# Small loads off the input's queue, one early layer-norm group, explicit attention buffers and fewer or more unread products in the seams

## The chip, the core and the metric

The kernel runs on one NeuronCore of a Trainium2 chip. The core has five engines that run side by side and wait for each other through semaphores: TensorE (PE, matrix products into PSUM), VectorE (DVE), ScalarE (ACT), GpSimd (POOL) and SyncE (SP, which here only starts DMAs). DMAs can be started by SP, ACT and POOL; each of the three has a queue of its own, and an engine issues its instructions in order. The metric is the device time of one execution in microseconds (us), over several runs.

## The reference

The input x is one image of 256 x 256 positions with 32 channels. Four layers follow, each adding its result to x; each first applies a group norm (16 groups of two channels, mean and variance over the whole image).

```
x = x + L0(_gn(x))     # layer norm over 32 channels, then attention
    a = softmax(a, axis=2)
    o = g * einsum('bstih,bsihc->bsihc', a, v)   # g = sigmoid(mn @ Wg), v = mn @ Wv
    o @ Wo + bo
x = x + L1(_gn(x))     # 3x3 average, then Sobel magnitude sqrt(gx^2 + gy^2 + eps)
x = x + L2(_gn(x))     # the same again
x = x + L3(_gn(x))     # two-layer LSTM-like recurrence, 256 sequences of 256 steps
```

In the einsum of layer 0 the softmax weights are summed over the very axis along which they add up to one, so attention is `g * v`: Wq and Wk don't reach the result. Layer 3 needs the group norm of the whole image before its first step.

## The kernel before

All 64 blocks of four image columns lie in SBUF as `xa`, 128 partitions (4 columns x 32 channels) by 256 rows. The work is done on 32 pairs of blocks (128 x 512 elements), in stages:

1. **Load** (lines 187 to 259). SP loads x in two halves of 16 columns and seven tiles `nat` of 32 columns, two DMAs each (L200). PE turns each pair with four transposes (L248), ACT copies it to `xa` (L255), DVE takes its statistics (L256). In the same SP queue, after the fourth tile, stand sixteen small loads (L205, L210): the layer norm's gamma and beta and the weights wv and wg, each four times for the four partition groups; and after all of x the constants kt (L211), mean_of (L213) and two rows for a later test (L721, L722). POOL's queue has bo, bout (L114) and wo (L126). POOL copies mean_of into `avg` (L217), then scales wv and wg by gamma (L221); PE multiplies the scaled weights (L228, L239) after the seventh tile of x.
2. **Group norm and layer norm** (lines 265 to 377). DVE aggregates the statistics (L267), PE averages them over groups (L270, L278), and DVE subtracts the mean from each pair (`shifted`, L285). Eight groups of four pairs follow: PE centres (L347), ACT squares (L370), PE sums the squares of the group before into `pvar`, one PSUM bank (L328). Groups below EARLY = 2 get their root and reciprocal ahead of the others, inside group EARLY + 1 at its third square (L338, L361); right there SP starts the DMAs that spread rows 0 to 2 of the reciprocal over partitions (`rows`, L306, four DMAs per pair), DVE shifts the last four pairs, does `norm_test` (L730 to L733), and the first three pairs are scaled (`scaled`, L316, on DVE for pair 0, else on POOL). The other groups' reciprocal (L377) comes after the last group.
3. **Attention** (lines 380 to 502). For each pair k, a list `plan` gives a time for every operation: eight gate products g and eight value products v (L432, 32 rows of PE each), ACT's sigmoid `sg` (L441), DVE's `mu` = (v + bias) x sg (L445), the output products `pr` and `pb` (L458), the residual `r` (L473, L474) and the statistics (L477). All pairs' operations are sorted by k x 5.9 + time and issued in that order. The sg tiles come from a pool of 8 buffers, the mu results `o` from one of 11. PSUM banks are handed out by `take` from a list of free ones. SP's DMAs for rows of pair 3 onward (`spread_out`) and the loads of the recurrent weights (L744, L749) are in its queue behind the first rows.
4. **Two Sobel layers** (lines 515 to 695). Each begins with `shift`: DVE aggregates (L554), PE averages the mean (L556) and the variance (L564). `busy(n)` puts n products of 128 x 256 ahead of, between and behind them; their results are read by nobody (L552). Then pairs pass through fifteen operations by a list of times; `mixed` is PE's part (L639), `residual` adds to the image (L656).
5. **The seam and the recurrence** (lines 702 to 1212). `group_norm` (L150 to L169), again with unread products (L140), then `finish` (L859 to L899), which makes the recurrence's bias rows: `sb` from the scale (L861) and the bias (L864), products `pgs` (L869), ACT's copy fx (L876), DVE's three-part split to fb (L882, L884), and pk (L889, L890). Then 256 steps whose order is a list of times with period 7.6; at its head two unread products (L1152), then the first bias products (L1037, L1040).

Stages 1 to 3 lie in one region in which every engine keeps the order of the program (`manual_schedule`), each Sobel layer and the recurrence in one of their own; `group_norm` and `finish` of stage 5 are outside, where a scheduler orders each engine's instructions.

Of the kernel before, what the change touches and what calls it, by code (L numbers as in the profile page):

```python
# [18 lines left out]
S = 256  # L19
T = 256  # L20
C = 32
# [40 lines left out]
def net_kernel(  # L62
# [47 lines left out]
    def per_channel(v, name):  # L110

        t = cp.tile([P, 1], F32, name=name)
        for j in range(J):
            nc.gpsimd.dma_start(out=t[j * C : (j + 1) * C, :], in_=v.rearrange("(c o) -> c o", o=1))  # L114
        return t

    gamma4 = cp.tile([P, 1], F32, name="gamma4")
    beta4 = cp.tile([P, 1], F32, name="beta4")
    bo4 = per_channel(b_o, "bo4")
    bout4 = per_channel(b_out, "bout4")  # L120

    wv4 = big2.tile([P, D], F32, name="wv4")
    wg4 = big2.tile([P, D], F32, name="wg4")
    wbias = cp.tile([P, 2, 2], F32, name="wbias")
    wo = cp.tile([P, D // P, C], F32, name="wo")
    nc.gpsimd.dma_start(out=wo, in_=w_o.rearrange("(k p) c -> p k c", p=P))  # L126
# [4 lines left out]
    def table(func, after):  # L131

        t = small.tile([P, 1], F32, name="table")
        nc.scalar.activation(t, after, func, scale=0.0, bias=one)
# [44 lines left out]


    avg = mp.tile([P, GROUPS, GROUPS, J], F32, name="avg")
    flag = cp.tile([1, 1], mybir.dt.int32, name="flag")
    stats = new_stats()
    def pair(t, k):
# [6 lines left out]
    with tc.tile_pool(name="nat", bufs=7, side="right") as natp, tc.tile_pool(  # L191
# [3 lines left out]
        for i, wl in enumerate(WIDTHS):  # L195
            name, bufs = ("nat", 7) if wl == 32 else ("half", 2)
            nat = natp.tile([P, 2, wl, C], F32, name=name, bufs=bufs)
            nats.append((nat, w0, wl))
            for h in range(2):
                nc.sync.dma_start(out=nat[:, h], in_=x_nat[:, h, w0 : w0 + wl, :])  # L200
            w0 += wl
            if i == 3:
                for t, v in ((gamma4, ln_gamma), (beta4, ln_beta)):
                    for j in range(J):
                        nc.sync.dma_start(  # L205
                            out=t[j * C : (j + 1) * C, :], in_=v.rearrange("(c o) -> c o", o=1)
                        )
                for t, w in ((wv4, w_v), (wg4, w_g)):
                    for j in range(J):
                        nc.sync.dma_start(out=t[j * C : (j + 1) * C, :], in_=w)  # L210
        nc.sync.dma_start(out=kt, in_=consts[:, 3:NK, :])  # L211
        mean_of = mp.tile([P, P], F32, name="mean_of")
        nc.sync.dma_start(out=mean_of, in_=consts[:, K_AVG, :])  # L213
        gb = norm_weights(tc, mp, gn_gamma, gn_beta)
        nc.gpsimd.memset(avg, 0.0)
        for g in range(GROUPS):
# [79 lines left out]
    def pair(t, k):  # L296
        return t[:, 2 * k : 2 * k + 2, :].rearrange("p b s -> p (b s)")

    EARLY = 2
    rstds = [lnp.tile([P, 2 * S], F32, name=f"rstd{i}") for i in range(2)]  # L300

    def rows_of(k):
# [15 lines left out]
    with tc.tile_pool(name="lnq", bufs=9) as lnq:  # L318
        with tc.tile_pool(name="ps_ln", bufs=7, space=PSUM) as ps_ln, tc.tile_pool(
# [22 lines left out]
            for g in range(GROUPS):  # L342
                pcs = [ps_ln.tile([P, 2 * S], F32, name="pc") for _ in range(J)]
                for j in range(J):
                    rows = slice(j * C, (j + 1) * C)
                    for r in range(J):
                        nc.tensor.matmul(  # L347
                            pcs[j][r * C : (r + 1) * C, :],
                            lhsT=cen[rows, rows],
                            rhs=pair(xb, J * g + r)[rows],  # L350
                            start=True,
                            stop=True,
                        )
                if g == 0:
                    for k in range(J, NST - J):
                        shifted(k)
                sqs = []
                for j, pc in enumerate(pcs):
                    if g == EARLY + 1 and j == 2:
                        std = deviations()  # L360
                        nc.vector.reciprocal(rstds[0], std)  # L361
                        for k in range(3):
                            rowsets[k] = rows_of(k)
                        for k in range(NST - J, NST):
                            shifted(k)
                        norm_test(tc, mp, flag, gb)
                        for k in range(3):
                            scaled(k)
                    sqs.append(lnq.tile([P, 2 * S], F32, name="sq"))
                    nc.scalar.activation(sqs[-1], pc, AF.Square)  # L370
                if g:
                    variance(g - 1, last)
                last = sqs
# [47 lines left out]
    with tc.tile_pool(name="at", bufs=3) as atp, tc.tile_pool(  # L421
        name="ps_at", bufs=1, space=PSUM
    ) as ps_at:
        free = list(range(8))
        held, sbuf = {}, {}

        def one_of(o, u, j, k):
            bias = lambda i: wbias[:, i, u : u + 1]
# [8 lines left out]
                    stop=True,  # L437
                )
            elif o == "sg":
                sg = sbuf["sg", u, j, k] = atp.tile([P, 2 * S], F32, name="sg", bufs=8)  # L440
                nc.scalar.activation(sg, held["g", u, j, k][1], AF.Sigmoid, bias=bias(1))  # L441
                release(("g", u, j, k))
            elif o == "mu":
                gated = sbuf["o", u, j, k] = atp.tile([P, 2 * S], F32, name="o", bufs=11)
                nc.vector.scalar_tensor_tensor(  # L445
                    gated,
                    held["v", u, j, k][1],
                    bias(0),
                    sbuf.pop(("sg", u, j, k)),
                    ALU.add,  # L450
                    ALU.mult,
                )
# [1 line left out]
            elif o in ("pr", "pb"):  # L454
                half = o == "pb"
                po = held["po", k][1] if half else take(("po", k))
                for i in range(J):
                    nc.tensor.matmul(  # L458
                        po[i * C : (i + 1) * C, :],
                        lhsT=wo[:, half, :],  # L460
                        rhs=sbuf.pop(("o", half, i, k)),
                        start=not half,
                        stop=half,
                    )
# [50 lines left out]
    def sobel_layer(src, dst, moments, before, after, between):  # L515
# [167 lines left out]
        with tc.manual_schedule():  # L683
            shift()
            for _, k, part, args in todo:
                part(k, *args)
                if part is twos and k == 0:
                    deviation()
                if part is statistics and between:
                    between.pop(0)(lambda: flat(ps_s.tile([P, 2, S], F32, name="pg1")))  # L690
        stack.close()
        return stats

    stats = sobel_layer(xa, xb, stats, 7, 16, [rw.selectors])
    stats = sobel_layer(xb, xa, stats, 3, 16, rw.products())
    second.close()

# [4 lines left out]
    inputs = RecurrentInputs(tc, ctx, xa)  # L702
    plain = nc.values_load(flag, min_val=0, max_val=1)
    with tc.tile_pool(name="ps_n", bufs=1, space=PSUM) as ps_n:
        gn = group_norm(stats, ps_n, 1, 0, 3)
        table(AF.Sigmoid, gn[0])
        weights = rw.finish(lw, ps_n, gn)
    with tc.If(plain > 0) as arms:
        recurrence(tc, out, ident, weights, inputs, None)
    with arms.Else():  # L710
# [25 lines left out]
class RecurrentWeights:  # L736
# [117 lines left out]
    def finish(self, lw, psum, gn):  # L854

        nc = self.nc


        for g in range(2):  # L859
            cols = slice(g * C, (g + 1) * C)  # L860
            nc.vector.tensor_scalar(  # L861
                self.sb[0:C, 0, cols], self.ident[0:C, 0:C], gn[0][0:C], None, ALU.mult
            )
        nc.vector.tensor_copy(self.sb[0:C, 1, :], gn[1][0:C].to_broadcast([C, 2 * C]))  # L864
        fx = lw.tile([P, G], F32, name="fx")
        pgs = [psum.tile([P, G], F32, name=f"pg{i}") for i in range(2)]
        for i in (1, 0):
# [103 lines left out]
def recurrence(tc, out, ident, weights, inputs, general):  # L971
# [222 lines left out]

    for k in range(inputs.NX, NB // inputs.XT):
        at(((k - inputs.NX + 1) * inputs.XT * J + 4.0) * PERIOD, inputs.load, k)
    at(-1e5, busy, 2)
    for n in range(min(ahead.values()), T + max(ahead.values())):
        at(n * PERIOD + OUT["x"], project, n)
    for t in range(T):  # L1200
# [53 lines left out]
```

## Time and profile before

| | us |
|---|---|
| median of 3 runs | 2545.38 (2543.13 to 2545.64) |
| the profiled execution | 2544.43 |
| its span, first to last instruction | 2542.6 |
| end of the load stage (last L255 copy) | 46.0 |
| attention's first product (L432) | 76.9 |
| first Sobel aggregation (L554) | 322.0 |
| second Sobel aggregation | 446.3 |
| aggregation before the recurrence (L150) | 573.5 |
| first product of the recurrence (L1037) | 586.7 |

The page of a profile gives the busy time of each engine and, in forty equal slices, the busy share in tenths; PEclk is the clock that TensorE was granted, in tenths of full speed, and DMA the busy share of the sixteen DMA engines. The chain that ended last is followed back from the last instruction, at each step to what released it. A line of a timeline has the start, the duration, the engine, the line of the kernel, the operation, its output and inputs, the count of merged instructions and, in brackets, how long the engine stood idle before it and what ended that. An engine's name with a q is its instruction queue, which issues DMAs. A product of 32-bit operands of 512 or 256 columns appears as two MATMUL instructions.

### The profile page before, as it was taken

Reading aid. Unit: us, or ns where it says so; the run is one execution under the profiler, and the core shown is the slowest. Engines: PE = TensorE matmul, PEld = TensorE weight load, DVE = VectorE, ACT = ScalarE, POOL = GpSimd, SP = SyncE. Lnnn points to the kernel's source line nnn. Section 1 sums busy time; section 2 is a strip of 40 time slices with the busy share of each in tenths; the row PEclk is TensorE's granted clock in tenths of the full one; section 3 lists DMA queues with packets and bytes.
Section 4 is the critical chain, followed back from the end, with each engine's and each line's share of the span. In section 5 each row is a group of like instructions: output and inputs, shape, how many; then the busy total and the mean of one; then the engine's idle time right before and its main releaser. Section 6 shows DMA issues by size and latency. Waiting matters only on the chain.

```text
span 2542.6 us, 41402 instructions
## 1 busy us (share of the span) xinstructions
PE 2478.7 (97%) x11567; PEld 1064.8 (42%) x11567; DVE 2275.0 (89%) x6635; ACT 2256.8 (89%) x6878; POOL 1324.9 (52%) x1352
## 2 busy tenths in 40 slices
PE   6899999998999999999999999999999999999997
PEld 4344355563444444444444444444444444444443
DVE  5688889886999999999999999999999999999997
ACT  5688867675999999999999999999999999999997
POOL 1234377773555555555555555555555555555553
PEclk8899999997999999999999999999999999999999
DMA  4777300001010101010101010010101010100000
GB/s 151 56 42 38 17 1 1 1 14 37 5 22 5 22 5 22 5 22 5 22 5 23 8 21 16 10 22 5 22 5 22 5 22 5 22 5 5 5 5 11
DMA packets 117704, 46.97 MB, mean 18 GB/s; under 512 B 77092, under 2 KB 110405, under 8 KB 117464
## 3 DMA queue, kind: packets, MB, share of 16 engines
q1 hardware_dynamic: 115944, 43.93, 12.9%
q8 instruction: 94, 1.54, 0.2%
q14 instruction: 146, 1.20, 0.2%
q10 hardware_dynamic: 1232, 0.26, 0.1%
q0 software_dynamic: 288, 0.03, 0.0%
HBM read 10.63 MB, written 8.39 MB: 7 GB/s over the span
## 4 chain that ended last, share of the span: by engine, by line
PE 94%; DMA 2%; DVE 1%; SPq 1%; ACT 1%; POOL 0%; issue 0%; POOLq 0%; DVEq 0%; ACTq 0%
PE zz L1072 36%; PE zz L1067 17%; PE zz L1040 9%; PE pg L639 9%; PE pa L432 6%; PE pt L1124 5%; PE zz L1037 3%; PE pa L458 2%; PE pt L1120 2%; PE px L1169 1%; PE px L1159 1%; PE pg L552 1%; DMA nat<-in_x_dram 1%; SPq L306 1%; DMA rows<-rstd 1%; DVE xb L285 1%
## 5 line engine op out<-in xcount | busy, mean ns | idle before, releaser
L1088 POOL TENSOR_TENSOR rs<-ve,mhalf 128x4 f32<-128x4 f32 x1024 | 1030.9, 1007 | 926.6 <-DVE ve L1085 926.6
L1072 PE MATMUL zz<-wc,hT 128*128 128x512 f32 x2040 | 1059.1, 607 | 1.3 <-DVE hT L1130 1.3
L1061 ACT ACTIVATE ga<-zz,rs 128x128 f32<-128x128 f32 x3072 | 972.9, 377 | 39.6 <-POOL rs L1088 10.5
L1085 DVE TENSOR_REDUCE ve<-sq 128x4 f32<-128x516 f32 x1024 | 704.2, 688 | 29.4 <-ACT sq L1080 7.0
L1080 ACT ACTIVATE sq<-zz 128x512 f32<-128x512 f32 x1024 | 629.2, 614 | 39.1 <-PE zz L1072 16.0
L1067 PE MATMUL zz<-wc,hT 128*128 128x512 f32 x1024 | 525.0, 594 | 0.0
L1072 PEld LDWEIGHTS zz<-wc,hT 128*128 128x128 f32 x2040 | 328.6, 190 | 399.3 <-DVE c L1116 167.6
L1061 ACT ACTIVATE go<-zz,rs 128x128 f32<-128x128 f32 x1024 | 394.0, 385 | 0.0
L1108 DVE TENSOR_TENSOR c<-ga 128x128 f32<-128x128 f32 x1024 | 299.8, 293 | 61.8 <-ACT ga L1061 32.0
L1116 DVE TENSOR_TENSOR c<-c,fc 128x128 f32<-128x128 f32 x1020 | 288.4, 283 | 9.0
L1112 DVE TENSOR_TENSOR fc<-ga,c 128x128 f32<-128x128 f32 x1020 | 292.4, 287 | 2.7 <-ACT ga L1061 2.7
L1040 PE MATMUL zz<-fx,xt 32*128 32x512 f32 x2048 | 266.6, 589 | 0.0
L441 ACT ACTIVATE sg<-pa,wbias 128x512 f32<-128x512 f32 x256 | 167.5, 686 | 56.4 <-DVE o L445 30.7
L445 DVE SCALAR_TENSOR_TENSOR o<-pa,wbias,sg 128x512 f32<-128x512 f32 x256 | 177.7, 744 | 31.6 <-ACT sg L441 20.7
L1124 PEld LDWEIGHTS pt<-ident,c 128*128 128x128 f32 x512 | 71.1, 139 | 284.9 <-DVE c L1116 276.3
L432 PE MATMUL pa<-xb,wg 32*128 32x512 f32 x512 | 167.0, 665 | 7.8 <-DVE xb L316 4.1
L1127 ACT ACTIVATE th<-c 128x128 f32<-128x128 f32 x512 | 166.2, 325 | 0.4 <-DVE c L1116 0.4
L1127 ACT ACTIVATE th<-pt 128x128 f32<-128x128 f32 x512 | 146.1, 285 | 19.0 <-PE pt L1124 19.0
L1067 PEld LDWEIGHTS zz<-wc,hT 128*128 128x128 f32 x1024 | 161.2, 197 | 2.8 <-issue 0.5
L1130 DVE TENSOR_TENSOR hT<-pt,th 128x128 f32<-128x128 f32 x512 | 146.3, 286 | 15.9 <-ACT th L1127 15.7
L432 PE MATMUL pa<-xb,wv 32*128 32x512 f32 x512 | 157.4, 651 | 0.0
L1120 PEld LDWEIGHTS pt<-ident,go 128*128 128x128 f32 x512 | 71.6, 140 | 203.4 <-ACT go L1061 202.9
(184 smaller groups left out, 2894.3 us busy)
## 6 DMA issues: line engine op xcount, KB each, us to landing
xt<-xa SPq DMA_DIRECT2D x256, 64.0 KB, 2.0
rows<-rstd SPq DMA_DIRECT2D x128, 64.0 KB, 6.6
out_dram<-st SPq DMA_DIRECT2D x252, 32.0 KB, 1.7
nat<-in_x_dram SPq DMA_DIRECT2D x14, 512.0 KB, 8.8
half<-in_x_dram SPq DMA_DIRECT2D x4, 256.0 KB, 3.5
wc<-in_L_conv_W_cell_dram SPq DMA_DIRECT2D x2, 512.0 KB, 6.1
kt<-in_consts_dram SPq DMA_DIRECT2D x1, 640.0 KB
kg<-in_consts_dram ACTq DMA_DIRECT2D x1, 128.0 KB, 3.2
```

What stands on the lines that cost most here:

```text
L432: nc.tensor.matmul(take((o, u, j, k)), lhsT=w[rows, u * P : (u + 1) * P], rhs=pair(xb, k)[rows], start=True, stop=True,)
L1040: nc.tensor.matmul(v["zz", l, h, t], lhsT=inputs.of(t, r), rhs=fx[r, :], start=False, stop=l == 0 and t == 0,)
L1061: nc.scalar.activation(dst, gates(x, g), func, scale=scale)
L1067: nc.tensor.matmul(get("zz"), lhsT=v["hT", 0, t][:, seqs], rhs=wc[:, l, 0, :], start=False, stop=t == 0)
L1072: nc.tensor.matmul(get("zz"), lhsT=v["hT", l, t - 1][:, seqs], rhs=wc[:, l, 1, :], start=False, stop=True,)
L1080: nc.scalar.activation(sqs[l, h, t % 2][:, :, 0:H], four(get("zz")), AF.Square, scale=float(H**-0.5))
L1085: nc.vector.tensor_reduce(ve, sqs[l, h, t % 2], AX.X, ALU.add)
L1088: nc.gpsimd.tensor_tensor(rs, get("ve"), inputs.mhalf, ALU.pow)
L1108: nc.vector.tensor_mul(c, gates(get("ga"), 0), gates(get("ga"), 2))
L1112: nc.vector.tensor_mul(fc, gates(get("ga"), 1), get("c"))
L1116: nc.vector.tensor_add(c, c, get("fc"))
L1127: nc.scalar.activation(th, get("pt")[:, 1, 0:P] if turned else get("c"), AF.Tanh)
```

## The change

- The sixteen small loads leave SP and are issued by POOL, ahead of bo, bout and wo; mean_of is issued by ACT, early.
- EARLY becomes 1: the first reciprocal covers only group 0 (pairs 0 to 3). Before it DVE shifts pairs up to 19, after it 20 to 31. It stands in group 2, at the second square.
- The sg and o tiles get a tag each, and the kernel hands them out itself from lists of free ones, first freed first used.
- The first Sobel layer has three unread products ahead of its mean, as the second has; both Sobel layers get seven more after their last `mixed`. `group_norm` before the recurrence has 3, 1 and 2 instead of 1, 0 and 3; the recurrence begins with three instead of two.
- `group_norm` and `finish` before the recurrence go into a `manual_schedule` region, and the bias copy goes ahead of the two scalings.

```diff
     gamma4 = cp.tile([P, 1], F32, name="gamma4")
     beta4 = cp.tile([P, 1], F32, name="beta4")
+    wv4 = big2.tile([P, D], F32, name="wv4")
+    wg4 = big2.tile([P, D], F32, name="wg4")
+    for t, v in (
+        (wv4, w_v),
+        (wg4, w_g),
+        (gamma4, ln_gamma.rearrange("(c o) -> c o", o=1)),
+        (beta4, ln_beta.rearrange("(c o) -> c o", o=1)),
+    ):
+        for j in range(J):
+            nc.gpsimd.dma_start(out=t[j * C : (j + 1) * C, :], in_=v)
     bo4 = per_channel(b_o, "bo4")
...
     avg = mp.tile([P, GROUPS, GROUPS, J], F32, name="avg")
+    mean_of = mp.tile([P, P], F32, name="mean_of")
+    nc.scalar.dma_start(out=mean_of, in_=consts[:, K_AVG, :])
...
             w0 += wl
-            if i == 3:
-                for t, v in ((gamma4, ln_gamma), (beta4, ln_beta)):
-                    for j in range(J):
-                        nc.sync.dma_start(
-                            out=t[j * C : (j + 1) * C, :], in_=v.rearrange("(c o) -> c o", o=1)
-                        )
-                for t, w in ((wv4, w_v), (wg4, w_g)):
-                    for j in range(J):
-                        nc.sync.dma_start(out=t[j * C : (j + 1) * C, :], in_=w)
         nc.sync.dma_start(out=kt, in_=consts[:, 3:NK, :])
-        mean_of = mp.tile([P, P], F32, name="mean_of")
-        nc.sync.dma_start(out=mean_of, in_=consts[:, K_AVG, :])
...
-    EARLY = 2
+    EARLY = 1
...
                 if g == 0:
-                    for k in range(J, NST - J):
+                    for k in range(J, 5 * J):
                         shifted(k)
...
-                    if g == EARLY + 1 and j == 2:
+                    if g == EARLY + 1 and j == 1:
                         std = deviations()
                         nc.vector.reciprocal(rstds[0], std)
                         for k in range(3):
                             rowsets[k] = rows_of(k)
-                        for k in range(NST - J, NST):
+                        for k in range(5 * J, NST):
                             shifted(k)
...
+        slots = {name: list(range(n)) for name, n in (("sg", 8), ("o", 11))}
+
+        def slot(name):
+            n = slots[name].pop(0)
+            return n, atp.tile([P, 2 * S], F32, name=name, tag=f"{name}{n}", bufs=1)
+
+        def use(name, key):
+            n, t = sbuf.pop(key)
+            slots[name].append(n)
+            return t
...
-                sg = sbuf["sg", u, j, k] = atp.tile([P, 2 * S], F32, name="sg", bufs=8)
+                _, sg = sbuf["sg", u, j, k] = slot("sg")
...
-                gated = sbuf["o", u, j, k] = atp.tile([P, 2 * S], F32, name="o", bufs=11)
+                _, gated = sbuf["o", u, j, k] = slot("o")
...
-                    sbuf.pop(("sg", u, j, k)),
+                    use("sg", ("sg", u, j, k)),
...
-                        rhs=sbuf.pop(("o", half, i, k)),
+                        rhs=use("o", ("o", half, i, k)),
...
                 part(k, *args)
+                if part is mixed and k == NST - 1 and args == (0,):
+                    idle = ps_s.tile([P, 2, S], F32, name="pg1")
+                    for _ in range(7):
+                        nc.tensor.matmul(idle[:, 0, :], lhsT=ident, rhs=kg, start=True, stop=True)
...
-    stats = sobel_layer(xa, xb, stats, 7, 16, [rw.selectors])
+    stats = sobel_layer(xa, xb, stats, 3, 16, [rw.selectors])
...
-        gn = group_norm(stats, ps_n, 1, 0, 3)
-        table(AF.Sigmoid, gn[0])
-        weights = rw.finish(lw, ps_n, gn)
+        with tc.manual_schedule():
+            gn = group_norm(stats, ps_n, 3, 1, 2)
+            table(AF.Sigmoid, gn[0])
+            weights = rw.finish(lw, ps_n, gn)
...
+        nc.vector.tensor_copy(self.sb[0:C, 1, :], gn[1][0:C].to_broadcast([C, 2 * C]))
         for g in range(2):
             cols = slice(g * C, (g + 1) * C)
             nc.vector.tensor_scalar(
                 self.sb[0:C, 0, cols], self.ident[0:C, 0:C], gn[0][0:C], None, ALU.mult
             )
-        nc.vector.tensor_copy(self.sb[0:C, 1, :], gn[1][0:C].to_broadcast([C, 2 * C]))
...
-    at(-1e5, busy, 2)
+    at(-1e5, busy, 3)
```

More of the change, by code (lines that the diff above doesn't have):

```diff
@@ L118, in net_kernel @@
     beta4 = cp.tile([P, 1], F32, name="beta4")
+    wv4 = big2.tile([P, D], F32, name="wv4")
[8 more added lines that the diff above has]
+            nc.gpsimd.dma_start(out=t[j * C : (j + 1) * C, :], in_=v)
     bo4 = per_channel(b_o, "bo4")
     bout4 = per_channel(b_out, "bout4")
-    wv4 = big2.tile([P, D], F32, name="wv4")
-    wg4 = big2.tile([P, D], F32, name="wg4")
     wbias = cp.tile([P, 2, 2], F32, name="wbias")
```

## The prediction

> **What bounds the kernel now.** I read the page's row of slices first, then the chain that ended last, then the timeline of each seam, engine by engine. The chain is TensorE nearly throughout, but the recurrence after about 587 us, which the change leaves alone, carries most of it; only the first 600 us can move.
>
> ```profile
> PE   6899999998999999999999999999999999999997
> PEclk8899999997999999999999999999999999999999
> DMA  4777300001010101010101010010101010100000
> PE 94%; DMA 2%; DVE 1%; SPq 1%; ACT 1%; POOL 0%; issue 0%; POOLq 0%; DVEq 0%; ACTq 0%
> ```
>
> The slices where PE is not full are the first two (loading) and the tenth (the seam before the recurrence), and there the granted clock falls too. Next the SP queue's timeline, with three stretches of the stage table (columns: window; its length; busy us and instructions of PE, PEld, DVE, ACT, POOL; clock; DMA share; GB/s), and the chain there.
>
> ```profile
> 2.62 1.88 SPq L200 DMA_DIRECT2D nat<-in_x_dram  x4
> 4.55 4.08 SPq L205 DMA_DIRECT2D gamma<-in_L_conv_ln_gamma_dram  x4
> 9.65 4.36 SPq L205 DMA_DIRECT2D beta<-in_L_conv_ln_beta_dram  x4
> 17.77 5.59 SPq L200 DMA_DIRECT2D nat<-in_x_dram  x10
> ...
> 14.00:16.00 2.00, 2.00 (x13) 2.00 (x12) 1.56 (x3) 1.46 (x3) 0.00 (x0) 1.00 0.13 33
> 26.00:28.00 2.00, 2.00 (x20) 1.88 (x18) 1.84 (x4) 1.99 (x5) 0.00 (x0) 1.00 1.02 414
> 34.00:36.00 2.00, 0.00 (x0) 0.00 (x0) 0.00 (x0) 0.00 (x0) 0.00 (x0) 0.50 0.10 34
> ...
> 25.61 10.41 DMA mean_of<-in_consts_dram
> 38.18 2.13 PE pt L239 x4
> ```
>
> From 4.55 to 17.77 us SP issues sixteen small loads (the wv and wg ones fill 14.05 to 17.73) while the input waits behind them: the DMA engines run at 0.13 where they can run at 1.02. Then PE stands still for 7.16 us because mean_of, behind the whole input and kt on SP, lands at 36.02; POOL needs it for avg, and only then scales the weights that PE multiplies at L239.
>
> The layer norm (VectorE), one attention block (VectorE, ScalarE), and the seam before the recurrence (PE and VectorE):
>
> ```profile
> 62.25 3.35 DVE L361 RECIPROCAL rstd<-std 128x512 f32<-128x512 f32 x1
> 76.06 0.69 DVE L316 TENSOR_TENSOR xb<-xb,rows 128x512 f32<-128x512 f32 x1 [5.04 <-DMA rows<-rstd]
> 76.67 3.35 DVE L377 RECIPROCAL rstd<-std 128x512 f32<-128x512 f32 x1
> ...
> 253.46 4.23 DVE L445 SCALAR_TENSOR_TENSOR o<-pa,wbias,sg 128x512 f32<-128x512 f32 x6 [0.81 <-ACT sg L441]
> 254.31 1.28 ACT L441 ACTIVATE sg<-pa,wbias 128x512 f32<-128x512 f32 x2 [0.88 <-DVE o L445]
> ...
> 576.02 0.42 PE L153 MATMUL pm<-mv,kg 128*128 128x1 f32 x2
> 579.41 3.68 PE L869 MATMUL pg<-bc,sb 33*64 33x512 f32 x8
> 583.14 0.69 DVE L882 CAST part<-pg 128x512 bf16<-128x512 f32 x1 [3.20 <-PE pg L869]
> 586.74 0.60 PE L1037 MATMUL zz<-fb,sel 32*128 32x512 bf16 x2
> ```
>
> **Loads.** Gone from SP: 13.2 us ahead of the last ten nat loads. All eighteen input loads are then issued by 0.73 + 18 x 0.47 = 9.2 us. About 3.2 MB had landed by 12 us (the two-microsecond windows from 2 to 12 us); the other 5.2 MB, with 0.3 MB of weights, take 13.4 us at 410 GB/s, so x is in by 25.5 us. The compute then sets the pace: twelve of the 32 pairs are through at 17.6 us as now; in 25.71 to 32 us ten pairs ran at ACT 0.51 and DVE 0.60 us each. Twenty pairs x 0.60 = 12.1 us, plus 2.1 us for the weight products (L228 took 1.04 at full clock, L239 2.13 at half), ends at 31.8 instead of 45.98: **-14.2 us**.
> Two rules speak against this. The Trainium skill, "DMA: Bandwidth & Descriptors", section "Issuing engines are not separate DMA queues", says that spreading loads over engines saves only the issue time, usually small, as all share the same 16 DMA engines. By it the gain would be near 0 on the input; the row shows 13.2 us of issue with the engines at 0.13, so I take the row. "TensorE: Matmul & The Clock Gate", Part 4, says the full clock doesn't engage for transposes. By it pairs stay at the slow 0.857 us and the stage ends at 12.0 + 28 x 0.857 + 2.5 = 38.5, a gain of 7.5. Here transposes were granted 1.00 at 26 to 30 us and ran at 273 ns, so I take 14.2 and keep 7.5 as the low end.
> What is moved past: on POOL sixteen more DMAs stand before bo, bout, wo, one, avg and the scaling. At 0.49 us each (the bout row) that is 7.8 us; at wo's 0.77 it is 12.3. POOL's first stretch then ends at 15 to 19 us instead of 7, the avg copies and two scalings (1.05 + 1.83) at 18 to 22, while PE asks for them at about 25. So they cost nothing; without that cover each microsecond late is one on PE. ident is made by POOL at 2.19 to 2.50 behind one DMA and is first needed at 4.2; I assume that place stays. mean_of goes to ACT's queue, one issue of 0.41 us (the kg row) before ACT's first copy at 5.69.
>
> **Layer norm.** With one early group VectorE has 17 shifts (0.46 each) before the reciprocal, not 25, so from 50.84 it is free at 58.66; std needs only group 0's variance and one square of group 2, at 58.1. The first reciprocal starts 3.6 us sooner. Moved behind it: twelve shifts, ending 67.55 on the old clock; PE's groups 5, 6 and 7 want theirs at 63.9, 66.1 and 68.3, and they are done at 63.9, 65.7 and 67.5, so no loss but also no slack. The single pvar bank now makes the second variance wait for std (56.7 to 58.15), with group 3 queued behind; the later wait at 60.80 (1.84 us) goes in its place. norm_test (3.8 us) follows at 71.3, still ahead of rows 0, which land 10.4 us after their first issue, at 72.4. Block 0's scaling, the second reciprocal behind it (76.67, now 73.5) and the twelve row DMAs all come about 3.5 us earlier. Blocks 4 to 7 now need the second reciprocal, but their rows are issued after 91 us on the old clock, so that costs nothing. SP's next waits (wc, bc, rows of block 3) follow the rows. **-3.5 us**, between -2.5 and -4.5: half clock holds in parts of 77 to 104 us, and its windows will fall otherwise.
>
> **Attention tiles.** In plan order with eight sg slots handed out first freed, first used, the sg of unit (0,0) takes the slot just read by mu (1,2) of the block before. The trace shows exactly that: mu (1,2) runs 253.46 to 254.20, and sg starts at 254.31. So before hands them out in the same order and I cost this at **0**. The loop of these two waits (0.81 and 0.88) sets the 6.95 us block. If it did open, PE's six groups of 0.99 to 1.07 would bound a block at about 6.26: -0.69 x 28 = -19. If sg waited for one mu more, 0.705 x 28 = +20.
>
> **Seams.** First: the old seven products (14 instructions) take 3.26 us and end at 324.6, the aggregate was ready at 323.0; three end at 322.8. PE's mean product comes at 323.05: **-1.4**. Second: PE falls idle at 442.6 for 3.1 us, the clock goes to half, and the three products take 2.90 instead of 1.4; mean at 448.39 where the aggregate was ready at 447.34. Seven products after the last Sobel product fill 442.6 to 445.85, against the release of the banks at 445.70, costing 0.15 at most: **-1.0**, or 0 if the clock drops anyway.
> Third: clock 0.50 holds from about 572 to 603. If it holds full, the mean product runs at 574.6 (aggregate ready 574.54), not 576.02, so std at 576.2, not 577.77. The bias copy now goes ahead of the two scalings, and pg[1] is multiplied first, at 577.0 instead of 579.41; its half is done after 0.9 us, not behind all eight in 3.68. part starts at 578.2, not 583.14; the four steps to fb take 2.72, so fb is at 580.9. busy's third product (6 x 0.23) starts when rest frees the banks, 579.8, and ends 581.2. So L1037 starts at 581.2 against 586.74: -5.5, and -0.9 more if the first L1040 products run at full clock. At half clock all through: mean product still late by up to 1.4, busy 2.6 us long, L1037 at 583.4 or later: -3. The two pk products now follow pg on PE, then the branch into the loop, which I can't price: 0 to 1.6 us (the idle ahead of L1152). I take **-5.5**, from -2 to -7.
>
> **Sum.** -14.2 - 3.5 + 0 - 1.4 - 1.0 - 5.5 = -25.6. The profiled execution took 2544.43 (span 2542.6 and 1.8 around it), so 2518.8; the median of the runs lies 0.95 above it: 2519.8.
>
> **Rivals.**
> *Load stage at the slow pace, or the weights late on POOL*: 7.5 gained there, not 14.2: 2526.5. For: the first pairs did run at 0.857. Against: the clock at 26 us. Chance 0.19.
> *The hand-out opens the loop*: 2519.8 - 19 = 2500.8. For: the two waits are on the block's loop. Against: 0.11 us after mu (1,2). Chance 0.06.
> *Slower*: the hand-out puts sg behind mu (0,1), two mu later, 1.41 x 28 = +39, 2559. It decides above 0.91 us a block (25.6/28). Nothing in the trace speaks for it. Chance 0.03.
> *The seam products don't hold the clock* (the change doesn't do what it says): 1.0 and 2.5 of the gain lost, 2523.3. This lies inside the forecast's own 2513 to 2525, chance 0.68 with it. Unnamed rest 0.04.
>
> **Range.** 2513 to 2529 takes in the forecast and nearly all of the slow-load case, 0.85; leaving out the open loop and the slower case. A measurement of this kernel tells about 0.2%, 5.1 us, from no change. Faster 0.95 (all but the slower case and half of the rest), same 0.02, slower 0.03.
>
> **What would show it.** Right: SP issues nat without a break to about 9 us, no gap of PE ahead of L239, the last L255 copy ends near 32 us; the first rows are issued some 16 us after that copy, now 19.6; the blocks still lie 6.95 us apart; PE passes from the last Sobel product to the junk products without a gap, at clock 1.00; L1037 starts some 8.4 us after the last residual's end, now 14.0. Wrong: wgam or beta landing after PE asks, transposes at 0.857 a pair, blocks further or less apart, clock 0.50 from the last residual on.

## The result and the profile after

The changed kernel takes 2520.43 us (median of 4 runs, 2519.08 to 2522.59); the kernel before, beside it, 2544.80 (4 runs, 2543.13 to 2545.64). The ratio is 0.9906 with a 95% interval of 0.9889 to 0.9923: 24.4 us faster, where the prediction said 25.6 less, 2519.8. The execution profiled after took 2522.59, the slowest of its four, with a span of 2520.8 us. In the lines below L210 is line 210 of the changed kernel; in the section on the experiments, of that run's own kernel. Three rows of slices from its page, and the chain by engine:

```profile
PE   7999999999999999999999999999999999999997
PEclk9899999998999999999999999999999999999998
DMA  6777100010010101010100101010101010100000
PE 76%; DVE 0%; ACT 0%; issue 0%; POOL 0%; POOLq 0%; ACTq 0%; DVEq 0%
```

The second slice of PE is full now, and the clock's low slice ahead of the recurrence has gone from 7 to 8. The chain, in this trace, can be followed back only to the head of the recurrence at 560.24, so its 76% are the recurrence; what the change did before that is read from the timelines. The loading, in the timeline of SP, POOL, PE and ACT:

```profile
2.62 15.43 SPq L210 DMA_DIRECT2D nat<-in_x_dram  x14
8.73 0.98 POOL L128 DMA_DIRECT2D gamma<-in_L_conv_ln_gamma_dram  x2 [2.36 <-DMA wv<-in_L_conv_Wv_dram]
20.52 0.92 POOL L220 TENSOR_SCALAR wgam<-wv,gamma 128x256 f32<-128x256 f32 x1
25.59 1.13 PE L238 MATMUL pt<-wgam,kg 128*128 128x256 f32 x4
27.19 4.01 ACT L254 COPY xa<-pt 128x512 f32<-128x512 f32 x8
```

and in the stage table (window; length; busy us and instructions of PE, PEld, DVE, ACT, POOL; clock; DMA share; GB/s):

```profile
4.00:10.00 6.00, 3.94 (x15) 2.99 (x16) 1.39 (x2) 1.50 (x3) 3.36 (x7) 1.00 0.99 320
18.00:26.00 8.00, 7.33 (x63) 6.84 (x62) 7.84 (x14) 7.33 (x16) 4.29 (x14) 1.00 1.04 401
26.00:31.20 5.20, 4.21 (x36) 3.84 (x34) 4.55 (x8) 4.75 (x10) 0.00 (x0) 1.00 0.35 139
```

SP issues nothing but input up to 18.05 us, the DMA engines are full from 4 to 26 us, and PE's weight products (L238) carry no wait: the 7.16 us ahead of them are gone. POOL has the weights scaled at 22.35, 3.2 us before PE wants them. The last copy ends at 31.20 instead of 45.98. The layer norm, SP and VectorE:

```profile
44.06 3.34 DVE L360 RECIPROCAL rstd<-std 128x512 f32<-128x512 f32 x1
...
47.43 16.18 SPq L305 DMA_DIRECT2D rows<-rstd  x12
...
57.22 0.69 DVE L315 TENSOR_TENSOR xb<-xb,rows 128x512 f32<-128x512 f32 x1 [0.75 <-DMA rows<-rstd]
58.61 3.35 DVE L376 RECIPROCAL rstd<-std 128x512 f32<-128x512 f32 x1 [0.70 <-ACT std L337]
```

The first rows leave 16.2 us after the last copy, where it was 19.65. VectorE, which stood 5.04 us before block 0's scaling, now waits 0.75 there: the eight shifts that were moved behind the reciprocal fill time in which the rows are on their way. One block of the attention, VectorE and ScalarE:

```profile
200.35 4.23 DVE L454 SCALAR_TENSOR_TENSOR o<-pa,wbias,sg 128x512 f32<-128x512 f32 x6 [0.81 <-ACT sg L450]
201.19 1.29 ACT L450 ACTIVATE sg<-pa,wbias 128x512 f32<-128x512 f32 x2 [0.88 <-DVE o L454]
```

The same two waits, of the same length as before. The first and the second seam on PE, before:

```profile
321.37 3.26 PE L552 MATMUL pg<-kg,ident 128*128 128x256 f32 x14 [1.67 <-DVE xa L468]
...
445.70 2.90 PE L552 MATMUL pg<-kg,ident 128*128 128x256 f32 x6 [3.11 <-DVE xb L656]
448.39 0.42 PE L556 MATMUL pg<-mv,kg 128*128 128x1 f32 x2
```

and after:

```profile
303.00 1.53 PE L561 MATMUL pg<-kg,ident 128*128 128x256 f32 x6 [1.67 <-DVE xa L477]
304.69 0.38 PE L565 MATMUL pg<-mv,kg 128*128 128x1 f32 x2 [0.16 <-DVE mv L563]
...
422.86 3.29 PE L699 MATMUL pg<-kg,ident 128*128 128x256 f32 x14
427.74 0.38 PE L565 MATMUL pg<-mv,kg 128*128 128x1 f32 x2
```

In the first, three products end before the aggregate is there, and PE waits for it (0.16), not the other way round. In the second, the seven products fill the time to the statistics. The seam before the recurrence, PE and VectorE:

```profile
552.68 1.02 DVE L158 BATCH_NORM_AGGREGATE mv<-stats 128x2 f32<-128x192 f32 x1
553.76 0.38 PE L161 MATMUL pm<-mv,kg 128*128 128x1 f32 x2
556.18 1.93 PE L883 MATMUL pg<-bc,sb 33*64 33x512 f32 x8
557.31 0.69 DVE L896 CAST part<-pg 128x512 bf16<-128x512 f32 x1 [0.88 <-PE pg L883]
559.95 0.15 DVE L912 TENSOR_TENSOR cst<-pk,bout 128x1 f32<-128x1 f32 x1
560.24 2.76 PE L1166 MATMUL px<-xa,ident 128*128 128x256 f32 x6 [1.59 <-DVE cst L912]
562.93 0.60 PE L1051 MATMUL zz<-fb,sel 32*128 32x512 bf16 x2
```

Down to `part` all goes as worked out: it starts 4.63 us after the aggregate, where 4.68 was forecast. Then the three unread products at the recurrence's head (L1166; "the head" below) wait 1.59 us for `cst`, the output's constant, and take 2.76 us instead of 1.5. The first product of the recurrence (L1051) comes at 562.93.

The ledger of the two traces, in us:

| stretch | before | after | saved | predicted |
|---|---|---|---|---|
| start to last copy of the load | 45.98 | 31.20 | 14.78 | 14.2 |
| last copy to pair 3's scaling | 53.16 | 49.67 | 3.49 | 3.5 |
| attention, mean of 20 blocks | 7.078 | 7.076 | 0.0 | 0 |
| first seam, aggregate to its mean on ACT | 2.86 | 1.55 | 1.31 | 1.4 |
| second seam, the same | 2.54 | 1.49 | 1.05 | 1.0 |
| third seam, aggregate to first recurrent product | 13.22 | 10.25 | 2.97 | 5.5 |

The recurrence runs beside the old one at a constant distance: its 101st reduction stands 24.09 us earlier, the tenth from the end 24.37. In the profiled execution the last steps then lose 2.5 us: two pairs of products at half clock,

```profile
2499.09 1.83 PE L1081 MATMUL zz<-wc,hT 128*128 128x512 f32 x2
2500.72 1.92 PE L1086 MATMUL zz<-wc,hT 128*128 128x512 f32 x2
```

where a pair took 1.02 us in the step before, and slower last stores of the output (3.45 us for 2.53). So the two spans differ by 21.8 us and the medians by 24.4.

### The profile page after: what moved, and what is told of

It reads as the page before. It is cut to its first block, busy times and chain, and to the rows that moved or that the text cites. A ratio compares the mean times of both kernels' runs of the same rounds, so it can differ in the third digit from the quotient of the medians.

```text
span 2520.8 us, 41461 instructions
## 1 busy us (share of the span) xinstructions
PE 2476.7 (98%) x11593; PEld 1062.3 (42%) x11593; DVE 2273.3 (90%) x6635; ACT 2256.1 (89%) x6878; POOL 1332.8 (53%) x1368
## 3 DMA queue, kind: packets, MB, share of 16 engines
q8 instruction: 95, 1.56, 0.3%
## 4 chain that ended last, share of the span: by engine, by line
PE 76%; DVE 0%; ACT 0%; issue 0%; POOL 0%; POOLq 0%; ACTq 0%; DVEq 0%
PE zz L1086 37%; PE zz L1081 17%; PE zz L1054 9%; PE pt L1138 5%; PE zz L1051 3%; PE pt L1134 2%; PE px L1183 1%; PE px L1173 1%; POOL rs L1102 0%; DVE ve L1099 0%; ACT ga L1075 0%; ACT sq L1094 0%; PE px L1166 0%; DVE c L1122 0%; ACT go L1075 0%
## 5 line engine op out<-in xcount | busy, mean ns | idle before, releaser
L1075 ACT ACTIVATE ga<-zz,rs 128x128 f32<-128x128 f32 x3072 | 972.8, 377 | 39.8 <-POOL rs L1102 10.9
```

The costliest lines, as they stand in the source:

```text
L1075: nc.scalar.activation(dst, gates(x, g), func, scale=scale)
```

## The experiments

The theory is that of the prediction: each part gives its own share, at its own place, and only the loads, the layer norm and the seams give anything. The rivals: the loads' gain belongs to one of its two moves; the hand-out of tiles is worth something in the attention; the products in the seams do nothing. And one question of the third seam: why 3.0 and not 5.5. Each run has its own runs of the kernel before beside it, so times of different experiments are compared by their ratios to it (the interval, 95%, in brackets); the changed kernel's is 0.9906.

**The small loads alone**, the kernel before with the sixteen loads of gamma, beta, wv and wg on POOL, `mean_of` left on SP:

```diff
+        for j in range(J):
+            nc.gpsimd.dma_start(out=t[j * C : (j + 1) * C, :], in_=v)
...
-            if i == 3:
...
-                for t, w in ((wv4, w_v), (wg4, w_g)):
-                    for j in range(J):
-                        nc.sync.dma_start(out=t[j * C : (j + 1) * C, :], in_=w)
```

> The kernel before with only the sixteen small loads moved from SP to POOL; mean_of stays behind kt on SP. Theory (SP's issue held the input back): all of x lands some 7 us sooner, PE then waits for mean_of, which lands at about 29 us, so the last L255 copy ends near 36.5 us instead of 46.0 and the run is 9.5 us faster than before (8 to 11). Rival (the shared DMA engines set the pace, the small loads only change places): at most 2 us faster.

Measured: 2538.16 us against 2545.47 (ratio 0.9968, 0.9955 to 0.998). The load ends at 39.77, 6.2 us earlier, not 9.5, and the run is 7.3 us faster, below the 8 to 11 expected. The timeline of SP and PE:

```profile
19.21 0.33 SPq L212 DMA_DIRECT2D mean_of<-in_consts_dram  x1
32.30 2.13 PE L238 MATMUL pt<-wgam,kg 128*128 128x256 f32 x4 [7.81 <-POOL wgam L220]
```

`mean_of` is issued at 19.21 but lands 10.9 us later behind the full queue of input, and POOL's scaling waits for it. The freed queue gives its time to a wait of 7.81 us on PE, and the 2.13 us are L238 at half clock after that pause.

**`mean_of` alone**, on ACT's queue, the small loads left on SP:

```diff
+    mean_of = mp.tile([P, P], F32, name="mean_of")
+    nc.scalar.dma_start(out=mean_of, in_=consts[:, K_AVG, :])
...
-        nc.sync.dma_start(out=mean_of, in_=consts[:, K_AVG, :])
```

> The kernel before with only mean_of moved to ACT's queue, early; the small loads stay on SP. Theory (two separate waits): PE's wait of 7.16 us ahead of L239 is gone and the clock stays full there, the last L255 copy ends near 37.5 us, 8.5 us faster than before (7 to 9.5). Rival (PE's wait hid the arrival of the last two input tiles): those land after 36 us and the gain is under 4 us.

Measured: 2534.59 us against the same 2545.47 (0.9954, 0.9937 to 0.9971); load end 38.37, 7.6 us earlier (8.5 expected). The wait ahead of the weight products is gone; the one for the input stays, as SP and PE show:

```profile
18.57 5.50 SPq L202 DMA_DIRECT2D nat<-in_x_dram  x10
22.61 0.45 PE L248 MATMUL pt<-ident,nat 128*128 128x128 f32 x1 [5.25 <-DMA nat<-in_x_dram]
```

**Both moves, and nothing else of the change** (the two diffs above together):

> The kernel before with both moves of loads and nothing else of the change. Theory: the load stage ends at about 31.2 us and everything behind it is only shifted: 14.8 us faster than before (13.5 to 16), less than the sum of the two single moves, since each wait partly covers the other. Rival (the shift is eaten up later, where clock windows fall otherwise): under 11 us faster.

Measured: 2528.82 us against 2545.47 (0.9934, 0.9917 to 0.995), 16.7 less. The load ends at 30.25, 15.7 us earlier. The moves alone gave 6.2 and 7.6 at the load's end, together 13.8: joined they give about the sum, where I had expected less. The two waits aren't two paths of which the longer hides the other: they follow one another, and the first move alone runs into the second wait. That the pair gives more than the sum isn't shown: these are single traces, the nine kernels that have both moves end the load anywhere from 29.91 to 31.20, and by the medians the moves alone gave 7.3 and 10.9, more than the 16.7 of both (the four runs with `mean_of` alone spread over 9.8 us). From the load's end to pair 3's scaling it is 53.41 us, as before (53.16): the layer norm's 3.5 us don't come from the loads. The third seam, untouched here, took 13.86 us from the aggregate to the first reduction of the recurrence against 16.45 in the kernel before, and that is how the run comes out 16.7 less with 15.7 at the load.

**The layer norm undone**, the changed kernel with two early groups and the old places of the shifts:

```diff
-    EARLY = 1
+    EARLY = 2
...
-                    for k in range(J, 5 * J):
+                    for k in range(J, NST - J):
...
-                    if g == EARLY + 1 and j == 1:
+                    if g == EARLY + 1 and j == 2:
...
-                        for k in range(5 * J, NST):
+                        for k in range(NST - J, NST):
```

> The kernel after with EARLY back at 2 and the shifts back in their old order. Theory (the first reciprocal, with its row DMAs behind it, gates the first attention blocks): from the last L255 copy to the scaling of pair 3 on POOL 53.2 us instead of 49.7, as in the kernel before, and the run 3.5 us slower than after (2 to 5). Rival (the rows are late whatever the reciprocal does, or PE at half clock hides it): that stretch and the run within 1 us of after.

Measured: 2524.80 us against 2548.75 (0.9911, 0.9895 to 0.9928). Load end to pair 3's scaling is 53.66 us against 49.67: 4.0 us, the whole term, at its place. It is more than scatter: the five kernels with two early groups have 53.16 to 53.66 us there, the seven with one 49.48 to 50.05. The time as a whole doesn't show the 3.5 us that were expected: the ratio is hardly different from the changed kernel's. Its interval is 0.3% wide, 8 us, and the profiled execution's third seam fell 1.65 us shorter (11.19 from aggregate to first reduction, against 12.84).

**More sigmoid tiles**, the changed kernel with ten `sg` tiles in place of eight, to see whether the hand-out of tiles binds the block at all:

```diff
-        slots = {name: list(range(n)) for name, n in (("sg", 8), ("o", 11))}
+        slots = {name: list(range(n)) for name, n in (("sg", 10), ("o", 11))}
```

> The kernel after with ten sg buffers in place of eight (o keeps eleven), handed out in the same way. Theory (the loop of ACT waiting for a buffer that mu has to free, and mu waiting for ACT, sets the 6.95 us block): the wait of 0.88 us goes, a block takes 6.2 to 6.5 us and the run is 13 to 21 us faster than after. Rival (PE or its banks set the block and the loop only fills in): the block stays within 6.8 to 6.95 us, under 4 us faster.

Measured: 2510.73 us against 2545.47 (0.9868, 0.9851 to 0.9884). The block's mean over 20 blocks falls from 7.076 to 6.837 us (most blocks from 6.95 to 6.75), and from pair 3's scaling to the last but one of POOL's residual additions it is 205.8 us against 212.2: 6.4 us less, between the two expectations and so neither of them. The waits from 120 to 280 us (us in total, times, longest), after and with ten tiles:

```profile
ACT sg L450 <- DVE o L454: 22.5, 27, 0.9
```

```profile
PEld pa L441 <- ACT sg L450: 31.0, 71, 0.8
ACT sg L450 <- PE pa L441: 28.3, 48, 1.2
```

ScalarE's wait for a tile that VectorE still reads is gone from the list. In its place ScalarE waits for PE, and PE for the PSUM bank that ScalarE has yet to read. So the loop that the prediction named was the bound, but opening it doesn't lead to PE's own 6.26 us a block: it stops at 6.75. By these waits the exchange of banks is the next loop; no run with another use of the banks tests that. Of the 9.7 us below the changed kernel, 6.4 are the blocks; the rest is mostly the start of the recurrence and the tail, where the clock differs from run to run.

**Eleven and ten**, one more `sg` and one `o` less, with the constant's addition moved as in a run further down:

```diff
-        slots = {name: list(range(n)) for name, n in (("sg", 8), ("o", 11))}
+        slots = {name: list(range(n)) for name, n in (("sg", 11), ("o", 10))}
```

> The same with eleven sigmoid tiles and ten gated ones. If what is left in the block is the wait for PSUM banks and for the products themselves, no tile of either ring is missing, and the block stays at 6.75 us and the time within 1 us of the run with ten and eleven. If the gated tiles bind at ten, DVE's gating products are held until the output products give a tile back, PE's output products come later, and the block is longer: 6.85 us or more, 28 blocks by 0.1 us or more, at least 3 us slower than the run with ten and eleven.

Measured: 2534.51 us against 2545.14 (0.9962, 0.9948 to 0.9976), and a block of 7.61 us, 24 us slower than with ten and eleven. The waits of the same window:

```profile
ACT sg L450 <- PE pa L441: 41.3, 42, 1.6
DVE o L454 <- PE pa L467: 17.3, 21, 0.9
```

The second line is new: VectorE waits for the output products to read a gated tile. By it, the one `o` tile less costs 0.77 us a block, though this run changes both rings at once. The slower rival of the prediction (39 us, by 1.41 us a block) was of this kind, a tile that comes free too late, only in the other ring.

**Without the seven products** behind the last Sobel product:

```diff
-                if part is mixed and k == NST - 1 and args == (0,):
-                    idle = ps_s.tile([P, 2, S], F32, name="pg1")
-                    for _ in range(7):
-                        nc.tensor.matmul(idle[:, 0, :], lhsT=ident, rhs=kg, start=True, stop=True)
```

> The kernel after without the seven unread products at the end of each Sobel layer. Theory (they keep the clock full over the wait for the last residual): the clock falls at both ends; from the aggregation of the second layer to its m15 2.5 us instead of 1.5, and from the aggregation before the recurrence to the recurrence's first L1099 about 15.5 us instead of 12.8; 3.7 us slower than after (2 to 5). Rival (the clock at a seam goes by where its windows happen to fall): neither stretch longer by more than 0.5 us in a consistent way.

Measured: 2523.53 us against 2548.75 (0.9904, 0.9888 to 0.9921). PE in the second seam:

```profile
426.26 2.90 PE L561 MATMUL pg<-kg,ident 128*128 128x256 f32 x6 [3.12 <-DVE xb L665]
428.95 0.42 PE L565 MATMUL pg<-mv,kg 128*128 128x1 f32 x2
```

The pause is back (3.12), the three products take 2.90 instead of 1.56, and the aggregate's mean comes after 2.54 us instead of 1.49, as expected. The next Sobel layer, starting at half clock, is 1.3 us longer. In the third seam the expectation failed: without the products the aggregate to the first reduction took 12.07 us, not 15.5, and no longer than the changed kernel's 12.84. There the half clock fell on 554.9 to 558.3 alone and the head ran at full clock. Up to the head the products do save time in the third seam too: it starts 8.43 us after the aggregate without them and 7.56 with them. Against the run with two early groups, which has the products and whose head also ran at full clock, the first reduction is 0.88 us later (12.07 against 11.19). The changed kernel's 12.84 hides this, as its clock fell within the head. In the second seam all five traces without the seven products have half clock, and the seven traces with them have none from 92 to 550 us. The time as a whole can't be told from the changed kernel's.

**Without the head's three products:**

```diff
-    at(-1e5, busy, 3)
```

> The kernel after without the three unread products at the head of the recurrence. Theory (they begin late, behind cst, run at half clock for 2.76 us and stand in the way of the first bias products): from the aggregation before the recurrence to the first L1099 about 10.6 us instead of 12.8, and the run 2 us faster than after. Rival (they warm the clock for the first steps, which is worth more than their own time): the stretch to the first L1099 at least as short as in after only up to there, the first steps slower, the run not faster.

Measured: 2519.00 us against 2548.75 (0.9887, 0.9871 to 0.9904). The first recurrent product comes 7.66 us after the aggregate (10.25 with the head), the first reduction 10.57 after it, as expected; the next hundred reductions (25 steps) take 193.2 us, not 195.0. The run with two early groups, which has the head and kept the clock through it, also takes 193.2 for these, and 9.03 and 11.19 us to the two points. So the head costs more than it brings: 1.4 us at the first product and 0.6 at the first reduction, as its products stand between `fb` and the first product of the recurrence. The ratio's interval overlaps the changed kernel's, so the 2 us that were expected for the run are not shown by the times.

**The constant first**, the changed kernel with the two `pk` products left behind `pg` but `cst` added right after the first remainder, not after `fb` (the `pk` lines, which move up in the text with it, are left out here):

```diff
...
             left = rest
+            if i == 1:
+                nc.vector.tensor_add(cst4, pk, self.bout4)
...
-        nc.vector.tensor_add(cst4, pk, self.bout4)
```

> The kernel after with cst (L912) put right behind the first rest (L898) on VectorE, so that the last reader of the seam's PSUM banks ends 1 us sooner. Theory (my sum took the banks to be free when rest ends, but the products at the recurrence's head wait for cst too): those products start about 1.2 us sooner, still at full clock, and end near the end of fb; from the aggregation to the first L1099 10.0 to 10.8 us instead of 12.8, the run 2 us faster than after (1 to 3). Rival (the branch into the recurrence holds PE, not the banks): the products start where they did, within 0.3 us of 7.6 us after the aggregation's start, and nothing is gained.

Measured: 2518.28 us against 2548.75 (0.9885, 0.9868 to 0.9901). VectorE and PE in the seam:

```profile
558.56 0.15 DVE L913 TENSOR_TENSOR cst<-pk,bout 128x1 f32<-128x1 f32 x1
558.86 1.53 PE L1167 MATMUL px<-xa,ident 128*128 128x256 f32 x6 [0.34 <-DVE cst L913]
560.32 0.39 PE L1052 MATMUL zz<-fb,sel 32*128 32x512 bf16 x2
```

The head waits 0.34 us instead of 1.59, and starts 6.31 us after the aggregate where it was 7.56. The first recurrent product comes 7.77 us after the aggregate; my prediction had worked out 7.68 for it. With the wait for `cst` out of the way its picture of this seam is right. The first reduction comes 9.94 us after the aggregate. In the times this gain, too, is within the two intervals.

**Ten tiles and the constant first together:**

> The changed kernel with ten sigmoid tiles instead of eight and the constant's addition right behind the first remainder. If the two gains are of separate places they add: steady block 6.75 us and scaling to last use some 6.4 us less than in the changed kernel, last aggregation to first reduction of the recurrence 9.9 us instead of 12.8, median 2520.4 - 9.7 - 2.2 = 2508.5 (2506 to 2511). If the ten tiles' gain was in part the luck of the clock at the recurrence's start and in the tail (its part behind the blocks was 3.3 us), the sum is smaller: -6.4 - 2.2, 2511.8.

Measured: 2510.54 us against 2545.14 (0.987, 0.9854 to 0.9887), no less than the 2510.73 of the ten tiles alone. The block is 6.836 us, as with ten tiles, and the head starts 6.32 us after the aggregate, as in the last run, not 7.57: both gains are there. But PE shows

```profile
550.22 2.36 PE L1167 MATMUL px<-xa,ident 128*128 128x256 f32 x6 [0.34 <-DVE cst L913]
552.51 0.60 PE L1052 MATMUL zz<-fb,sel 32*128 32x512 bf16 x2
```

the clock going to half within the head. With ten tiles alone it also fell there, but for 3.4 and 6.8 us; here it stayed at half for 20.5. So the first reduction comes 11.85 us after the aggregate (12.71 with ten tiles alone, 9.9 expected), and the next hundred reductions take 195.0 us instead of 192.8. With ten tiles (with or without the constant) the kernel is the fastest seen here, about 10 us below the changed kernel, and its interval just clears that of the changed kernel.

## Why the prediction was right, and where it was not

**Loads, right: 14.78 for 14.2**, though three of its readings were off, and that two of the errors cancel is luck. The first is of SP's queue. SP was to have issued the input by 9.2 us at 0.47 us a load; it took to 18.05. From 12 us on an issue itself takes only 0.33 us. But by the trace's records eight semaphores go round among the loads of SP and ACT, and each load waits for the landing of the one eight before it; from 12.3 us on SP issues 0.02 us after that landing. SP's waits up to 30 us (us in total, times, longest), before and after:

```profile
SPq L205 <- DMA nat<-in_x_dram: 4.1, 4, 1.1
SPq L205 <- DMA half<-in_x_dram: 1.4, 1, 1.4
```

```profile
SPq L210 <- DMA nat<-in_x_dram: 7.0, 6, 1.6
```

So the 13.2 us in which the small loads held SP were not all issue time: those of gamma and beta (L205) stood 5.5 us waiting for input to land. Nor were the DMA engines at 0.13 throughout: they were at 0.78 to 0.99 up to 12 us and at 0.13 to 0.25 from 12 to 18, when the loads that SP had under way were nearly all small ones. After the change an input load stands in each of those places and the engines are full to 26 us, so SP's longer issuing cost nothing.

The other two readings are of the pace. By 17.6 us nine pairs were through, not twelve; in exchange the other 23 ran at ScalarE's 0.51 us a pair, not the 0.60 I took (17.3 + 23 x 0.51 + 2.2 for the weight products is 31.2). The slow pace of the first pairs is that of half clock: in the kernel before, copies stand 0.855 us apart at a recorded 0.50, too (24.00, 24.86, 25.71). The 1.00 that the tables show for the first pairs is no record: the trace's records of the clock begin at 17.68, in the kernel before at 15.62. In all twelve traces they begin with a 1.00 between 8.8 and 17.7 us, and there the transposes go from 0.21 us apart to 0.11.

Of the two rules weighed there, the Trainium skill's "Issuing engines are not separate DMA queues" ("DMA: Bandwidth & Descriptors"), that spreading the loads saves only issue time, was taken to give near 0; taking the sixteen small loads off SP gave 6.2 us alone and 8.1 on top of the other move (15.7 - 7.6), because the engines had been left idle, which the rule doesn't speak of. The rule of Part 4 in "TensorE: Matmul & The Clock Gate", no full clock for transposes, would have left the pairs at 0.857 us: eight ran in 4.01 us at clock 1.00, and the first 1.00 of each trace came while PE ran nothing but transposes. In both the row of the trace was the better guide.

**Layer norm, right: 3.49 for 3.5,** and undone it costs 4.0 at its place.

**Attention tiles, right: 0.** The two waits and the block are the same under the hand-out as under the ring: 6.95 us in most blocks of all four traces with the ring and all five with the hand-out of eight tiles. What the rival got wrong about an opened loop was the bound behind it: 6.75 us in the steady block with ten tiles, not 6.26, and the waits there point to PSUM banks going to and fro.

**First and second seam, right: 1.31 and 1.05 for 1.4 and 1.0.** The second is shown by taking the products out. The first rests on the ledger and on its repetition: 2.85 or 2.86 us in the four traces with seven products, 1.55 or 1.56 in the eight with three.

**Third seam, the term that was mis-sized: 2.97 for 5.5.** The step that failed is that of busy's third product: it "starts when rest frees the banks, 579.8". The head does wait for the banks, but `rest` isn't their last reader: `cst` is, which reads `pk` and which the change left on VectorE behind the four steps to `fb`. (The head's products don't use `cst`, and moving it moves them.) In the kernel before, `pk` came ahead of `pg`, and `cst` was added four us before the first remainder:

```profile
579.52 0.16 DVE L898 TENSOR_TENSOR cst<-pk,bout 128x1 f32<-128x1 f32 x1 [0.72 <-PE pk L890]
```

I had seen that the `pk` products now follow `pg`, and priced only PE's side of it, not whose turn it became on VectorE. That is 1.25 us of the head's start (7.56 after the aggregate, 6.31 with `cst` first), and as much at the first recurrent product: it comes 9.03 us after the aggregate in the run with two early groups, whose seam is the same and kept the clock,

```profile
564.41 1.53 PE L1166 MATMUL px<-xa,ident 128*128 128x256 f32 x6 [1.59 <-DVE cst L912]
565.88 0.39 PE L1051 MATMUL zz<-fb,sel 32*128 32x512 bf16 x2
```

and 7.77 with `cst` first, the head at full clock too. The other 1.22 us of the profiled execution (10.25 against 9.03) is the clock, gone to half at 560.40, within the head. The two make up the 2.5 us that were missing. That the seam's half clock is partly luck is shown by seams of the same code: the old one took 16.45, 16.46, 16.44 and 13.86 us from aggregate to first reduction in four kernels, the new one 12.84, 11.19 and 12.71. The mean gain is 3.6 us.

**The sum.** 25.6 was predicted and 24.4 measured. The load gave 0.6 more, the third seam some 2 less by its first reduction (3.6 us there), and the pieces between agree within 0.1 each. That the two misses partly cancel is luck, too.

What stays open: what decides where the half-clock stretches fall; what the new order of the bias rows gives apart from the unread products, as the two weren't run apart; and whether the head is worth its place once `cst` comes first. A pause of 1.59 us ahead of the head was followed by half clock in one run and not in another, and in the run with both changes half clock came after one of only 0.34.

## What to carry to other kernels

When two waits follow one another on the same path, taking away the first alone brings the work sooner to the second: moving the small loads gave 6.2 us with the wait for `mean_of` still there and 8.1 without it. When products are moved on one engine, look at what their reader does on the next: moving `pk` behind `pg` showed no cost on PE, and cost 1.25 us because VectorE then came to it last. When a queue is slow to issue, look at what each issue waits for before calling it issue time. Before a ring of tiles is made longer, find the loop behind it (here, by the waits, the PSUM banks), and count the ring next to it: ten and eleven tiles gained about 10 us, eleven and ten lost these and some 14 more.

## What the hardware showed that was not expected

- The granted clock in these traces changes only between 1.00 and 0.50, and the stretches at half are multiples of 3.41 us: 62.05 to 68.88, 560.40 to 563.81 and 567.2 to 580.9 after; 445.7 to 449.1 and 572.0 to 602.7 before. Within each of the twelve traces all changes lie on one grid of 3.41 us, which lies differently against the seams from trace to trace. Where they fall in a seam moves a run by 1 to 3 us, as much as several of the changes tried there.
- The 1.00 that a page shows ahead of the first record of the clock isn't measured; here the work up to it ran at the pace of half clock.
- POOL, issuing its many small loads, waited for its own earlier ones (2.36 us for wv's, ahead of its tenth load at 8.73, and again for 0.84 at 10.56). These waits are the program's: another eight semaphores go round among its loads, and the tenth waits for the second, landed at 8.45. POOL's scalings ended at 22.35 us; PE asked 3.2 us later, which is all the cover that was left.
